# Projections in pairs, statistics apart, transfers of the end spread, a second bank in the opening, output weights later

## The chip, the cores and the metric

The kernel runs on one core of a Trainium2 chip. The core has a matrix engine (TensorE, PE in the profile; PEld is its weight load), a vector engine (VectorE, DVE), a scalar engine (ScalarE, ACT), a general one (GpSimd, POOL) and a queue that issues transfers (SyncE, SP). Each works through its own list in order; waits between them go over semaphores. The metric is device time in microseconds (us), lower is better: the median of three runs was 3494.31 us (3493.81 to 3497.04).

## The reference

Two batches `b` of 2048 rows and 512 features go through two layers. The first is a state-space block with a feed-forward part. The second is attention with 16 heads of 32 features, without an MLP in what is returned:

```python
h = _sln(hidden, w, ...)                      # layer norm, then gamma * ln + beta
qkv = (h @ Wqkv.T + bqkv).reshape(B, N, num_heads, hd, 3)
energy = jnp.einsum('bhqd,bhkd->bhqk', q, k)
att = jax.nn.softmax(energy, axis=-1) / D ** 0.5
out = jnp.einsum('bhqk,bhkd->bhqd', att, v)
out = out @ Wp.T + bp
h1 = out + hidden
h2 = _sln(h1, w, ...)
return h2 + h1
```

`_sln` takes mean and variance of each row, so the output of a row needs all heads of that row first, then the projection with `Wp`, the residual, and the norm's statistics.

## The kernel before, in words

Everything is float32. Rows are worked in chunks of 512 (`CH`), four a batch, and tiles of 128 rows. The order on every engine is the order in which the program is written out (`manual_schedule`): there is no scheduler, and lists of due work decide what is placed where.

First part. For each of eight chunks `(b, c)` the state-space block of the next chunk, the feed-forward part of this one, and the attention's features of the one behind are interleaved. The features of a chunk become keys and queries (`at_heads`, L523 to L537, product `pk`) and values (`at_values`, L539 to L551, product `pv`), and go to DRAM (`kd`, `qd`, `vd`). A key or query piece is evacuated by `halves`: ACT makes `hi`, DVE makes `lo` from the same PSUM bank and `hi`. Transposed features (`pt_tf`, L149) are evacuated by ACT into `fT`. All these pieces take their PSUM bank from `Banks.tile` (L191 to L196), which goes round the pools in `banks`; after the first part one pool of one bank, `ps_a`, is left in it. `hi` has two buffers, `lo` one.

Second part. A block `n` is a batch, a pair of heads and a chunk of queries: 2 x 8 x 4 = 64 blocks (`blocks`; in batch 1 the last chunk of the last two pairs stands at the end). A block is worked in `NP` = 8 periods `j`; for the keys it has 16 tiles of 128. Of these, 11 (`NX`) are kept: PE makes scores `s` (L753), ACT copies them to a ring buffer `x` (L764), DVE takes the running maximum `run` (L769). The maxima over the other five tiles come from `m` (L778, one buffer) and `top` (L783). `turn_run` and `spread` (L785 to L808) make the largest values into a row and send it to all partitions by DRAM (`flat`, then `shift`). From then on POOL takes the shift off a kept tile (`take_off`, L812), or DVE makes a tile anew with the shift off (`make`, L818, `pT`), ACT takes the exponential (L823), and PE multiplies with the values and a column of ones (`weighted`, L833, `o`). Maxima run `AHEAD` = 14 periods before the exponentials. In a period PE makes one `m` pair, one or two kept tiles, at most one made tile, and the `o` of two tiles. At the end of a block `raw` goes to DRAM: sums to `sd` (L846), weighted values to `od` (L849).

The opening is where the two parts meet, periods -22 to -5: the pieces that are left of the first part (`left`: eight `at_values`, four `at_features`, eight `at_heads`) are placed between the maxima of blocks 0 and 1. In period -4 the pools of the first part are closed; the PSUM of the second is `ps` (pool `ps2`): two double banks `s`, one double bank `m`, one bank `pt` for transposes, and one for `o`.

Output tiles. When all heads of a chunk are done, sums are inverted (`fetch_sums`, `invert`) and each of its row tiles is fetched, divided by its sums on POOL, projected, and normed. For batch 0 this is spread over the blocks of batch 1, two tiles in three blocks: with `k` a multiple of 8, group by group of 128 features `project` is placed in periods `k+5`, `k+6`, `k+7` (before the `o` products) and `k+8` (at the period's start), then `residual` and `statistics` at the end of `k+8`, `gain` in `k+9`. The projection `py` uses the bank `pt`. For batch 1 a tile comes every two periods, with all four groups together; its row `y` has one buffer (L972), from which the result is sent out (L980).

The last chunk has its own path: `end_fetch` (L990 to L1012) loads what its tiles need into free ring buffers in period `j-1` with `j` = 504: products of heads (`o`), divisors (`by`, one transfer a head, `end_divisors`), rows of `x2` (`h`) and a turned copy of the last group of output weights (`w`, with `turn`). `end_divide`, `end_begin`, `end_project` and `end_last` use them from period 507 on. The output weights `wp` are loaded in period 2 and scaled on POOL in period 8 (L1219 to L1222).

All transfers named here are issued by SP in program order. The program's transfers rotate through eight semaphores, and one is not issued before the one eight places earlier has landed.

Of the kernel before, what the change touches and what calls it, by code (L numbers as in the profile page):

```python
# [11 lines left out]
HALF = mybir.dt.float32r  # L12
# [7 lines left out]
P = 128  # L20
# [19 lines left out]
def tile_s5_block_then_sln_attention(  # L40
# [21 lines left out]
    nc = tc.nc  # L62
    NB, L, D = x.shape
    KC = D // P
    CH = 512
    TT = CH // P
    NCH = L // CH
    FC = w1.shape[1] // P
    NH, HD = 16, 32
    NG = D // P  # L70
# [31 lines left out]
    x2 = [dpool.tile([L, D], F32, name=f"x2_{b}") for b in range(NB)]  # L102
# [4 lines left out]
    od = [dpool.tile([D, L], F32, name=f"od_{b}") for b in range(NB)]  # L107
    sd = [dpool.tile([NH, L], F32, name=f"sd_{b}") for b in range(NB)]
    invd = [dpool.tile([NH, L], F32, name=f"invd_{b}") for b in range(NB)]
# [45 lines left out]
    def halves(hi, lo, psum, bias):  # L155

        nc.scalar.activation(hi, psum, AF.Identity, bias=bias, scale=1.0)  # L157
        nc.vector.scalar_tensor_tensor(lo, psum, bias, hi.bitcast(F32), ALU.add, ALU.subtract)  # L158
# [21 lines left out]
    work1 = late.enter_context(tc.tile_pool(name="work", bufs=2))  # L180
    banks = [late.enter_context(tc.tile_pool(name="ps_a", bufs=1, space=PSUM))]
# [9 lines left out]
    class Banks:  # L191


        def tile(self, shape, dtype, name, tag=None):
            banks.append(banks.pop(0))
            return banks[-1].tile(shape, dtype, name=name, tag="ps")  # L196

    ones = Banks()

# [60 lines left out]
    for q in range(4):  # L260
        f = FC // 4
        cols = slice(q * f * P, (q + 1) * f * P)
# [260 lines left out]
    def at_heads(b, c, i):  # L523

        w, bias, dst = ((wk, V_BK, kd[b]), (wq, V_BQ, qd[b]))[i // KC]
        g, hT = i % KC, fts[b, c]
        at = slice(c * CH, (c + 1) * CH)
        pk = ones.tile([P, CH], F32, name="pk")
        for k in range(KC):
            nc.tensor.matmul(  # L530
                pk, w[:, k, g * P : (g + 1) * P], hT[:, k, :], start=k == 0, stop=k == KC - 1
            )
        hi = work1.tile([P, CH], HALF, name="hi")
        lo = work1.tile([P, CH], HALF, name="lo", bufs=1)
        halves(hi, lo, pk, vec[:, bias + g : bias + g + 1])
        nc.sync.dma_start(dst[0, g * P : (g + 1) * P, at], hi.bitcast(F32))
        nc.sync.dma_start(dst[1, g * P : (g + 1) * P, at], lo.bitcast(F32))  # L537
# [22 lines left out]
    spare = ps1.tile([P, TT, D], F32, name="spare", tag="po", bufs=1)  # L560
# [126 lines left out]
    for j in range(2 * KC):  # L687
        left.insert(TT + j, (at_heads, *order[-1], j))
# [15 lines left out]
    ring = ctx.enter_context(tc.tile_pool(name="ring", bufs=22, side="right"))  # L704
    rows_r = ctx.enter_context(tc.tile_pool(name="rows_r", bufs=2, side="right"))
    ps = ctx.enter_context(tc.tile_pool(name="ps2", bufs=1, space=PSUM, side="right"))
    dsum = ctx.enter_context(tc.tile_pool(name="dsum", bufs=3, space=DRAM))

    ISQ = 1.0 / float(D) ** 0.5
# [10 lines left out]
            opens.append(n)  # L720
    pair_of = [pairs.index((b, p)) for b, p, _ in blocks]
    kst, qst, shifts, runs, tops = {}, {}, {}, {}, {}
    kept, probs, outs, ends = {}, {}, {}, {}

    def load_k(i):
        b, p = pairs[i]
# [258 lines left out]
    LB, LC = NB - 1, NQ - 1  # L985

    def spare(name):
        return ring.tile([P, 2, CH], F32, name=name, tag="x")

    def end_fetch():  # L990
        cols = slice(LC * CH, (LC + 1) * CH)
        ends["o"] = [spare("o01"), spare("o23")]
        ends["by"] = [spare("by01"), spare("by23")]
        ends["h"] = [spare("h01"), spare("h23")]
        w = spare("w")
        ends["w"], ends["turn"] = w[:, 0, :], w[:, 1, :P]
        for g in range(NG - 1):
            nc.sync.dma_start(ends["o"][g // 2][:, g % 2, :], od[LB][g * P : g * P + P, cols])
            end_divisors(range(4 * g, 4 * g + 4))
        for t in range(TT):  # L1000
            at = slice((LC * TT + t) * P, (LC * TT + t + 1) * P)
            nc.sync.dma_start(ends["h"][t // 2][:, t % 2, :], x2[LB][at, :])
        nc.gpsimd.tensor_copy(ends["turn"], ident)

        for to, of in ((0, 2), (1, 0), (2, 1), (3, 3)):
            nc.sync.dma_start(
                ends["w"][HD * to : HD * to + HD, :], wp[HD * of : HD * of + HD, NG - 1, :]
            )
        for to, of in ((0, 1), (3, 2)):
            nc.gpsimd.tensor_copy(  # L1010
                ends["turn"][:, HD * to : HD * to + HD], ident[:, HD * of : HD * of + HD]
            )  # L1012

    def end_fetch_more():
        cols = slice(LC * CH, (LC + 1) * CH)
        nc.sync.dma_start(ends["o"][1][HD : 3 * HD, 1, :], od[LB][D - P : D - P // 2, cols])

    def end_divisors(heads, shift=0):
        cols = slice(LC * CH, (LC + 1) * CH)
        for j in heads:  # L1020
            at = slice(HD * (j % 4 + shift), HD * (j % 4 + shift) + HD)
            nc.sync.dma_start(
                ends["by"][j // 8][at, j // 4 % 2, :], invd[LB][j : j + 1, cols].to_broadcast([HD, CH])
            )

    def end_divide(g, rows=slice(0, P)):
        o, by = ends["o"][g // 2][rows, g % 2, :], ends["by"][g // 2][rows, g % 2, :]
# [77 lines left out]
    NP = 8  # L1105
# [19 lines left out]
    def after(j, what, *args):  # L1125

        due.setdefault(j, []).append((what, args))

    def closing(j, what, *args):

        due.setdefault(j + 0.5, []).append((what, args))
# [13 lines left out]
    for b in range(NB):  # L1145
        for c in range(NQ):
            j = NP * (blocks.index((b, NPAIR - 1, c)) + 1) + 1
            if (b, c) == (LB, LC):
                most, rest = slice(0, NH - 4), slice(NH - 4, NH - 2)
                j = NP * (N - 1)  # L1150
                after(j - 5, fetch_sums, b, c, most)
                after(j - 3, invert, b, c, most)
                after(j - 1, end_fetch)
                after(j + 1, end_fetch_more)
                after(j + 1, fetch_sums, b, c, rest, 32)
                after(j + 4, invert, b, c, rest, 32)
                after(j + 5, end_divisors, range(NH - 4, NH - 2), 1)
                for g in range(NG - 1):
                    after(j + 3 + g, end_divide, g)
                for e in (1, 2):  # L1160
                    after(j + 8, end_divide, NG - 1, slice(HD * e, HD * e + HD))
                after(j + 6, end_begin, 0)
                for g in range(NG - 1):
                    after(j + 6 + g // 2, end_project, 0, [g])
                continue
            after(j, fetch_sums, b, c)
            after(j + 2, invert, b, c)
            if c == 0:
                after(j + 2, last_rows, b) if b == LB else after(NP * (NPAIR * NQ * (b + 1) + 2), last_rows, b)
            for t in range(TT):  # L1170
                qt = c * TT + t
                if b == LB:
                    k = j + 3 + 2 * t
                    after(k, fetch, b, qt)
                    after(k + 2, divide, b, qt)
                    after(k + 3, project, b, qt)
                    after(k + 3, residual, b, qt)
                    after(k + 3, statistics, b, qt)
                    after(k + 4, deviation, b, qt)
                    after(k + 5, last_norm, b, qt)  # L1180
                    after(k + 6, last_close, b, qt)
                else:

                    k = NP * (NPAIR * NQ * (b + 1) + 2 + 3 * qt // 2)
                    after(k, fetch, b, qt)
                    after(k + 3, divide, b, qt)
                    for g in range(3):
                        closing(k + 5 + g, project, b, qt, (g,))
                    after(k + 8, project, b, qt, (3,))
                    closing(k + 8, residual, b, qt)  # L1190
                    closing(k + 8, statistics, b, qt)
                    closing(k + 9, gain, b, qt)
                    after(k + 11, turns, b, qt)
                    closing(k + 12, scaled, b, qt)
                    after(k + 14, close, b, qt)
# [5 lines left out]
    def block_at(j):  # L1201
        n, i = divmod(j, NP)
        return (n, i) if 0 <= n < N else (None, i)

    for j in range(FIRST, NP * N + 2):
        if j == OPEN:
# [5 lines left out]
            rows = ctx.enter_context(tc.tile_pool(name="rows", bufs=2))  # L1212
# [3 lines left out]
            for v in vst:  # L1216
                nc.gpsimd.memset(v[:, :, 1, :], 1.0)
            wp = fixed.tile([P, KC, D], F32, name="wp")
        if j == 2:  # L1219
            nc.sync.dma_start(wp, w_pT.rearrange("(k p) f -> p k f", p=P))  # L1220
        if j == NP:
            nc.gpsimd.tensor_scalar(wp, wp, ISQ, None, ALU.mult)  # L1222
        run_due(j)
        n, i = block_at(j + AHEAD)
        todo = list(keeps[i]) if n is not None else []
        now, k = block_at(j)
# [24 lines left out]
        n, i = block_at(j + 1)  # L1251
# [4 lines left out]
        n, i = block_at(j - 1)  # L1256
# [59 lines left out]
```

## Time and profile before

| | |
|---|---|
| median of three runs | 3494.31 us |
| profiled execution, own time | 3497.08 us |
| its span, first to last instruction | 3495.3 us |
| mean granted TensorE clock | 0.989 |
| first part, to the last `po` product | about 1384 us |
| opening, to the first transposed row of maxima | 1384 to 1473 us |
| plain blocks of the second part | 28.5 us each |
| blocks 33 to 57, with output tiles of batch 0 | 29.5 to 35.5 us each |
| blocks 61 and 62, with output tiles of batch 1 | 49.1 and 48.6 us |
| chain that ended last, by engine | PE 73%, DVE 13%, ACT 8%, DMA 2%, POOL 2% |

How it is read: busy time is given by engine and by line; a group's line names what is written and read. In the timeline, each row has its start in us from the span's start, its duration, engine, line and tile; the bracket says how long the engine was idle before it and what released it. The waits list who waited for whom: us in total, times, longest. Matmuls overlap, so the distance between starts, not the duration, is what PE spends: a projection of one group is two rows, 0.43 us apart each.

### The profile page before, as it was taken

How to read it: one execution, taken by the hardware profiler on the slowest of the kernel's cores; microseconds unless marked ns; L12 is line 12 of the kernel's file. 1: busy time of each engine (PE TensorE's matmuls, PEld its weight loads, DVE VectorE, ACT ScalarE, POOL GpSimd, SP SyncE). 2: the span in 40 equal slices, each digit the busy share in tenths (PEclk: the TensorE clock that was granted, in tenths of full speed). 3: DMA queues.
4: the chain of work that ended last, by engine and by line, in shares of the span. 5: the costliest groups of instructions: out<-in, count | busy, mean ns of one | idle time of the engine just before them, and what ended most of it. 6: DMA issues, size and time to landing. Idle time of an engine off the chain costs nothing.

```text
span 3495.3 us, 34359 instructions
## 1 busy us (share of the span) xinstructions
PE 3343.7 (96%) x11764; PEld 1509.3 (43%) x11764; DVE 2153.1 (62%) x2976; ACT 1942.2 (56%) x2208; POOL 2137.7 (61%) x1162
## 2 busy tenths in 40 slices
PE   7999999999999999799999999999999999999997
PEld 4444444444444444444444444444444444444432
DVE  6232232323232311488888888888888888888885
ACT  2111111111111011389999999999888888888862
POOL 4223131313131310189899989998889888889986
PEclk8999999999999999999999999999999999999999
DMA  8001111111111112322223232323233233233233
GB/s 301 1 30 42 43 42 43 42 48 39 46 39 37 39 36 66 115 67 68 62 57 72 66 74 51 74 67 74 61 91 86 70 86 83 67 84 81 56 104 105
DMA packets 201638, 237.06 MB, mean 68 GB/s; under 512 B 89786, under 2 KB 118970, under 8 KB 197368
## 3 DMA queue, kind: packets, MB, share of 16 engines
q1 hardware_dynamic: 201464, 234.87, 24.6%
q8 instruction: 93, 1.52, 0.2%
q14 instruction: 81, 0.66, 0.1%
HBM read 166.77 MB, written 67.76 MB: 67 GB/s over the span
## 4 chain that ended last, share of the span: by engine, by line
PE 73%; DVE 13%; ACT 8%; DMA 2%; issue 2%; POOL 2%; SPq 0%; DVEq 0%; ACTq 0%; POOLq 0%
PE o L833 15%; PE ph L487 13%; PE po L500 13%; PE s L753 10%; DVE run L769 9%; PE pk L530 6%; ACT x L764 4%; PE pv L542 3%; PE py L904 3%; PE m L778 3%; PE pt_run L789 2%; PE pu L421 2%; ACT x L823 1%; ACT pT L823 1%; PE pt_tf L149 1%
## 5 line engine op out<-in xcount | busy, mean ns | idle before, releaser
L812 POOL TENSOR_TENSOR x<-x,shift 128x1024 f32<-128x1024 f32 x704 | 1654.1, 2390 | 159.9 <-DMA shift<-flat 135.8
L764 ACT COPY x<-s 128x1024 f32<-128x1024 f32 x704 | 692.4, 1012 | 212.8 <-PE s L753 211.6
L769 DVE TENSOR_TENSOR run<-s,run 128x1024 f32<-128x1024 f32 x576 | 703.0, 1220 | 82.0 <-ACT x L764 59.0
L823 ACT ACTIVATE x<-x 128x1024 f32<-128x1024 f32 x704 | 739.6, 1060 | 14.7 <-POOL x L812 14.5
L833 PE MATMUL o<-x,v 128*64 128x512 f32 x2816 | 720.4, 613 | 0.0
L753 PE MATMUL s<-qs,ks 128*128 128x512 f32 x2048 | 670.0, 422 | 50.4 <-DVE run L769 44.9
L487 PE MATMUL ph<-fT,w_sb 128*128 128x512 f32 x1024 | 463.1, 596 | 0.0
L500 PE MATMUL po<-w_sb,hid 128*128 128x512 f32 x1024 | 460.3, 592 | 0.0
L753 PEld LDWEIGHTS s<-qs,ks 128*128 128x128 f32 x2048 | 335.2, 189 | 274.0 <-DVE run L769 173.8
L783 DVE TENSOR_REDUCE top<-m 128x1 f32<-128x640 f32 x512 | 417.7, 816 | 40.7 <-PE m L778 38.1
L818 DVE TENSOR_TENSOR pT<-s,shift 128x1024 f32<-128x1024 f32 x320 | 389.5, 1217 | 57.6 <-PE s L753 57.6
L491 ACT ACTIVATE hid<-ph,vec 128x512 f32<-128x512 f32 x128 | 88.0, 687 | 595.7 <-PE ph L487 595.7
L823 ACT ACTIVATE pT<-pT 128x1024 f32<-128x1024 f32 x320 | 339.4, 1060 | 67.3 <-DVE pT L818 67.3
L158 DVE SCALAR_TENSOR_TENSOR lo<-pk,vec,hi 128x512 fp32r<-128x512 f32 x64 | 48.1, 751 | 505.2 <-ACT hi L157 500.0
L833 PE MATMUL o<-pT,v 128*64 128x512 f32 x1280 | 333.5, 600 | 13.4 <-ACT pT L823 13.4
L833 PEld LDWEIGHTS o<-x,v 128*64 128x64 f32 x2816 | 157.3, 136 | 316.7 <-issue 214.4
L487 PEld LDWEIGHTS ph<-fT,w_sb 128*128 128x128 f32 x1024 | 193.1, 192 | 228.7 <-issue 228.7
L778 PE MATMUL m<-ks,qs 128*128 128x320 f32 x1024 | 261.5, 337 | 29.1 <-DVE top L783 25.7
L434 POOL TENSOR_TENSOR m<-m,m 128x512 f32<-128x512 f32 x8 | 13.1, 1641 | 449.7 <-DVE m L432 449.7
L500 PEld LDWEIGHTS po<-w_sb,hid 128*128 128x128 f32 x1024 | 190.7, 190 | 221.4 <-issue 221.4
L157 ACT ACTIVATE hi<-pk,vec 128x512 fp32r<-128x512 f32 x64 | 44.0, 687 | 394.1 <-PE pk L530 389.5
L510 POOL TENSOR_TENSOR x<-x,gated 128x512 f32<-128x512 f32 x32 | 39.6, 1270 | 354.3 <-DVE gated L509 354.3
(253 smaller groups left out, 2781.8 us busy)
## 6 DMA issues: line engine op xcount, KB each, us to landing
ks<-kd SPq DMA_DIRECT2D x128, 256.0 KB
qs<-qd SPq DMA_DIRECT2D x512, 64.0 KB
shift<-flat SPq DMA_DIRECT2D x64, 512.0 KB
x<-in_x SPq DMA_DIRECT2D x8, 1024.0 KB
w_sb<-in_w SPq DMA_DIRECT2D x8, 1024.0 KB
x<-x SPq DMA_DIRECT2D x8, 1024.0 KB
kd<-hi SPq DMA_DIRECT2D x32, 256.0 KB
kd<-lo SPq DMA_DIRECT2D x32, 256.0 KB
```

The costliest lines, as they stand in the source:

```text
L487: nc.tensor.matmul(ph, w1_sb[:, k, f * P : (f + 1) * P], fts[b, c][:, k, :], start=k == 0, stop=k == KC - 1)
L500: nc.tensor.matmul(pos[b, c][:, t, :], hid[:, t * P : (t + 1) * P], w2_sb[:, f, :], start=f == 0, stop=f == FC - 1,)
L530: nc.tensor.matmul(pk, w[:, k, g * P : (g + 1) * P], hT[:, k, :], start=k == 0, stop=k == KC - 1)
L753: nc.tensor.matmul(s[:, e, :], kst[pair_of[n], e][:, kt * P : (kt + 1) * P], qst[n][:, e, :], start=True, stop=True,)
L764: nc.scalar.copy(x, s)
L769: nc.vector.tensor_tensor(runs[n], s, kept[n, 0] if kt == 1 else runs[n], ALU.max)
L778: nc.tensor.matmul(m[:, i, :YW], qst[n][:, e, t * P : (t + 1) * P], kst[pair_of[n], e][:, k : k + YW], start=True, stop=True,)
L783: nc.vector.tensor_reduce(tops[n][:, j, 0:1], m[:, :, :YW], AX.XY, ALU.max, negate=True)
L812: nc.gpsimd.tensor_tensor(x, x, shifts[n], ALU.add)
L818: nc.vector.tensor_tensor(x, s, shifts[n], ALU.add)
L823: nc.scalar.activation(x, x, AF.Exp)
L833: nc.tensor.matmul(outs[n][64 * e : 64 * e + 64, :], v[:, kt, e : e + 2, :], x[:, e, :], start=first, stop=final,)
```

## The change

- `Banks.tile`: the pool `ps2` is appended to `banks`, with the tag `pt`, so the pieces of the opening go in turn to `ps_a` and to the bank `pt`.
- `lo` gets the two buffers of its pool.
- Batch 0's tiles: two groups of the projection in period `k+5` and two in `k+6`, all at the period's end; `residual` at the end of `k+7`, `statistics` at the end of `k+8` as before.
- `end_fetch` is cut in three. `end_sums(g)` loads `o` and `by` of one group, in periods 502, 503 and 504. `end_weights` makes `w` and `turn` in 505, `end_x` loads `h` in 506. The divisors of four heads are one transfer with a repeated source instead of four, the two of the last heads one instead of two, and the four of `h` become two.
- `wp` is loaded in period 22 and scaled in period 32.

```diff
@@ Banks.tile
-            return banks[-1].tile(shape, dtype, name=name, tag="ps")
+            return banks[-1].tile(shape, dtype, name=name, tag="pt" if banks[-1].name == "ps2" else "ps")
@@ at_heads
-        lo = work1.tile([P, CH], HALF, name="lo", bufs=1)
+        lo = work1.tile([P, CH], HALF, name="lo")
@@ after the pool ps2
+    banks.append(ps)
@@
-    def end_fetch():
+    def end_sums(g):
+        if g % 2 == 0:
+            ends["o"].append(spare("o4"))
+            ends["by"].append(spare("by4"))
         cols = slice(LC * CH, (LC + 1) * CH)
-        ends["o"] = [spare("o01"), spare("o23")]
-        ends["by"] = [spare("by01"), spare("by23")]
+        nc.sync.dma_start(ends["o"][g // 2][:, g % 2, :], od[LB][g * P : g * P + P, cols])
+        end_divisors(g, 4)
+
+    def end_x():
         ends["h"] = [spare("h01"), spare("h23")]
+        at = slice(LC * CH, (LC + 1) * CH)
+        rows = x2[LB][at, :].rearrange("(i t p) d -> p i t d", p=P, t=2)
+        for i in range(2):
+            nc.sync.dma_start(ends["h"][i], rows[:, i, :, :])
+
+    def end_weights():
         w = spare("w")
         ends["w"], ends["turn"] = w[:, 0, :], w[:, 1, :P]
-        for g in range(NG - 1):
-            nc.sync.dma_start(ends["o"][g // 2][:, g % 2, :], od[LB][g * P : g * P + P, cols])
-            end_divisors(range(4 * g, 4 * g + 4))
-        for t in range(TT):
-            at = slice((LC * TT + t) * P, (LC * TT + t + 1) * P)
-            nc.sync.dma_start(ends["h"][t // 2][:, t % 2, :], x2[LB][at, :])
...
-    def end_divisors(heads, shift=0):
+    def end_divisors(g, heads, shift=0):
         cols = slice(LC * CH, (LC + 1) * CH)
-        for j in heads:
-            at = slice(HD * (j % 4 + shift), HD * (j % 4 + shift) + HD)
-            nc.sync.dma_start(
-                ends["by"][j // 8][at, j // 4 % 2, :], invd[LB][j : j + 1, cols].to_broadcast([HD, CH])
-            )
+        nc.sync.dma_start(
+            ends["by"][g // 2][HD * shift : HD * (shift + heads), g % 2, :],
+            invd[LB][4 * g : 4 * g + heads, cols].unsqueeze(1).to_broadcast([heads, HD, CH]),
+        )
@@ placement of the end
-                after(j - 1, end_fetch)
-                after(j + 1, end_fetch_more)
+                for g in range(NG - 1):
+                    after(j - 2 + g, end_sums, g)
+                after(j + 1, end_weights)
+                after(j + 1, end_sums_more)
+                after(j + 2, end_x)
...
-                after(j + 5, end_divisors, range(NH - 4, NH - 2), 1)
+                after(j + 5, end_divisors, NG - 1, 2, 1)
@@ placement of batch 0's tiles
-                    for g in range(3):
-                        closing(k + 5 + g, project, b, qt, (g,))
-                    after(k + 8, project, b, qt, (3,))
-                    closing(k + 8, residual, b, qt)
+                    for g in range(NG):
+                        closing(k + 5 + g // 2, project, b, qt, (g,))
+                    closing(k + 7, residual, b, qt)
                     closing(k + 8, statistics, b, qt)
@@ output weights
-        if j == 2:
+        if j == 2 * NP + 6:
             nc.sync.dma_start(wp, w_pT.rearrange("(k p) f -> p k f", p=P))
-        if j == NP:
+        if j == 4 * NP:
             nc.gpsimd.tensor_scalar(wp, wp, ISQ, None, ALU.mult)
```

More of the change, by code (lines that the diff above doesn't have):

```diff
@@ L722, in tile_s5_block_then_sln_attention @@
     kst, qst, shifts, runs, tops = {}, {}, {}, {}, {}
-    kept, probs, outs, ends = {}, {}, {}, {}
+    kept, probs, outs, ends = {}, {}, {}, {"o": [], "by": []}
     def load_k(i):
@@ L1012, in end_fetch, with end_sums_more @@
             )
-    def end_fetch_more():
+    def end_sums_more():
         cols = slice(LC * CH, (LC + 1) * CH)
         nc.sync.dma_start(ends["o"][1][HD : 3 * HD, 1, :], od[LB][D - P : D - P // 2, cols])
-    def end_divisors(heads, shift=0):
+    def end_divisors(g, heads, shift=0):
         cols = slice(LC * CH, (LC + 1) * CH)
-        for j in heads:
-            at = slice(HD * (j % 4 + shift), HD * (j % 4 + shift) + HD)
-            nc.sync.dma_start(
-                ends["by"][j // 8][at, j // 4 % 2, :], invd[LB][j : j + 1, cols].to_broadcast([HD, CH])
-            )
+        nc.sync.dma_start(
+            ends["by"][g // 2][HD * shift : HD * (shift + heads), g % 2, :],
+            invd[LB][4 * g : 4 * g + heads, cols].unsqueeze(1).to_broadcast([heads, HD, CH]),
+        )
     def end_divide(g, rows=slice(0, P)):
```

## The prediction

> **What bounds the kernel now.** I read the page first, then the waits of TensorE (PE) by stretch, then the timeline where a wait is large, then the waits of the SyncE queue (SP).
>
> ```profile
> span 3495.3 us, 34359 instructions
> PE 3343.7 (96%) x11764; PEld 1509.3 (43%) x11764; DVE 2153.1 (62%) x2976; ACT 1942.2 (56%) x2208; POOL 2137.7 (61%) x1162
> ```
>
> PE is the bound over the whole, so the change is worth the PE idle time it removes, plus slow-clock time that this idle brings. Four places.
>
> Opening, 1384 to 1475 us: the last pieces of the feed-forward part are worked off beside the first keeps of the attention. Waits of PE there (us in total, times, longest):
>
> ```profile
> PE pk L530 <- DVE lo L158: 9.4, 7, 1.6
> PE pv L542 <- ACT vt L547: 3.2, 3, 1.8
> PE pt_tf L149 <- ACT fT L150: 2.9, 2, 1.9
> ...
> PE pv L542 <- DVE lo L158: 0.3, 1, 0.3
> ```
>
> Every piece waits for the evacuation of the one before: there is one bank. Together 15.8 us.
>
> Block 1, timeline:
>
> ```profile
> 1513.18 5.37 POOL L1222 TENSOR_SCALAR wp<-wp 128x2048 f32<-128x2048 f32 x1
> ...
> 1521.03 1.06 ACT L823 ACTIVATE x<-x 128x1024 f32<-128x1024 f32 x1 [4.51 <-POOL x L812]
> ...
> 1524.30 1.22 PE L753 MATMUL s<-qs,ks 128*128 128x512 f32 x2 [3.94 <-DVE run L769]
> ```
>
> The scaling of `wp` on POOL makes ACT, then PE, idle. The issues of `sd<-raw` close the blocks: 1516.5, 1552.2, 1580.7, 1609.2. Block 1 takes 35.65 us, the plain ones 28.52: a loss of 7.1, of which 3.9 is the idle; the rest goes with a granted clock of 0.50 in 1524 to 1528.
>
> Batch 0's output tiles, 2490 to 3230, PE's waits and one tile:
>
> ```profile
> PE m L778 <- DVE top L783: 21.0, 15, 1.4
> ```
>
> ```profile
> 2790.93 0.69 DVE L914 TENSOR_TENSOR py<-py,xr 128x512 f32<-128x512 f32 x1
> ...
> 2795.07 0.56 PE L778 MATMUL m<-ks,qs 128*128 128x320 f32 x2 [1.40 <-DVE top L783]
> ...
> 2796.86 1.94 PE L833 MATMUL o<-x,v 128*64 128x512 f32 x4
> ...
> 2822.40 0.82 DVE L783 TENSOR_REDUCE top<-m 128x1 f32<-128x640 f32 x1 [1.74 <-PE m L778]
> ```
>
> Residual and statistics stand together in DVE's queue after the runs of period 8; the next `top` is late and `m` has one buffer: 1.4 us once a tile. In three tiles (about 2540, 2796 and 3086) the clock drops after it; four `o` matmuls take 1.94 instead of 1.08. The last line shows DVE idle ahead of period 8's own `top`.
>
> End:
>
> ```profile
> 3415.48 0.43 SPq L998 DMA_DIRECT2D o<-od  x1
> ...
> 3430.07 0.53 SPq L980 DMA_DIRECT2D out<-y  x1
> ...
> 3433.88 0.69 DVE L973 TENSOR_TENSOR y<-z,g_row 128x512 f32<-128x512 f32 x1 [10.87 <-DMA out<-y]
> ...
> 3439.01 1.98 PE L833 MATMUL o<-pT,v 128*64 128x512 f32 x4 [8.69 <-ACT pT L823]
> ```
>
> `end_fetch` issues 3+12+4+4 = 23 transfers from 3415.48 to 3429.97. `out<-y`, whose data POOL had ready at 3421.55, is behind them; `y` has one buffer, so DVE's next `y` waits, and the `pT` behind it, and PE.
>
> **The Trainium skill.** "Perfetto Trace Analysis", Matmuls, says that independent groups should rotate through PSUM banks so that one's evacuation overlaps the next's matmuls; the 1.56 us gaps of `pk` agree. "TensorE: Matmul & The Clock Gate", What's actually happening, says that the clock halves after an idle window of about 3.4 us that runs free; the halves after 3.94 and, phase permitting, after 1.40 us of idle agree. "DMA: Bandwidth & Descriptors", Why a DMA increments its semaphore by 16 and not by 1, says that a transfer uses as many engines (up to 16) as divide both slowest dimensions: the merged `by` (4 heads outermost) would use 4. With Specifications' 27 GiB/s an engine, 256 KB are an estimated 2.3 us plus latency; no trace shows it yet.
>
> **The change part by part.**
>
> Two banks in the opening. Removed: 15.8 us of waits. Kept: `pk` needs all four `fT`. From the fourth `pv` ACT has three copies (1.0 each) and four `fT` (0.78) to do, 6.1 us; PE's own work there is about 1.0 shorter. New: the second bank is that of `pt_run`. In the order, a `pv` now stands after `pt_run` 0 and has to wait for its `top` (vt 0.69 and top 0.68, less 1.0 of m and s between them: 0.35), and `pt_run` 1 waits for that `pv`'s evacuation (latency 0.2, vt 0.69: 0.95). 15.8 - 1.0 - 1.3 = 13.5. The order of ACT, DVE and SP is the same in this stretch; DVE has 3.5 us of work per two pieces (lo 0.75 twice, top 0.81, run 1.22) against PE's 7.9 (eight issues of 0.43 a piece, m and s 1.1). Bounds: 5 if the writes of `hi` and `lo` (the first took up to 5 us to land) hold the two buffers, 15 if nothing new waits. The second buffer of `lo` removes one cause, a wait at 1421.00. Taken: -13.5.
>
> `wp` later. Load and scaling move to periods 22 and 32, POOL's queue keeps two take-offs of block 4 ahead of the scaling. Block 1's loss of 7.1 goes. In block 4 POOL starts at 1599.78, two take-offs at 2.39 end at 1604.6, the scaling at 1610.0, the third at 1612.4; ACT wants it at 1609.08. So ACT is 3.3 late, PE about 0.6 less (4.51 against 3.94 in block 1): 2.7, and a slow window of 2.5 with it: 5.2. The cover is POOL's early start, 1.2 us better than in block 1 because no `ks` loads follow the shift. On SP the 1.32 us issue of `wp` comes right after block 3's `shift` and ahead of the `v` loads, which have 9 periods; sharing the engines could hold `shift` up as `ks` loads do (5.4 us of POOL idle against 2.8), at most 0.4 late for ACT. Bounds: 7.1 gain (hidden) to 1 loss. Taken: -1.9.
>
> Projections. PE work is the same, 8 issues of 0.43; two groups stand in period 5 and two in 6. The residual moves ahead of `top` in period 8. There DVE is idle for 1.74; the last group no longer delays `m`, which takes 0.86 off; 0.88 is left, the residual needs 0.69, so it is hidden. If that cover is gone it costs 0.69. After the runs DVE then has 0.69 less: `m` waits 0.7, not 1.4. 16 x 0.69 = 11.0. Without 1.4 us gaps I expect the three slow windows to go; each costs four or eight `o` at double time, some 1.7: 5.1, of which I take 4. Bounds: 0 to -16. Taken: -15.
>
> End. Now 2 issues in each of periods 502 and 503, so `out<-y` is ready to go at its data, 3421.6, and lands by 3425.4 (3.8 as above). The next `y` can run at 3425.5 (its `z` ends at 3425.41), the residual at 3427.1 (PE's `py`), after statistics `pT` at 3429.2 and its exponential to 3431.5; PE resumes at 3431.6, not 3439.0: 7.4. The slow clock after it (`o` 1.98 for 1.08, `py` 4.25 for 3.70) goes: 1.4. In exchange the following `out<-y` stands behind `o`, `by`, the four `w` (0.6 each) and waits for `od<-raw`; I put it at 3432.5, landed at 3436.3, 1.3 after its `y` is wanted, where before that wait was 4.1. The two 512 KB `h` have four periods. POOL's `turn` copies (0.64) move two periods down, under the same slack. Bounds: 2 to 11. Taken: -8.7.
>
> Sum: -13.5 - 1.9 - 15 - 8.7 = -39.1. The profiled execution took 3497.08 (its span and 1.8 around it): 3458. The median is 2.8 below it: 3455, which I round up for parts counted whole: **3456**.
>
> **Rivals.**
>
> A. The opening finds another wait: the landings of `hi`/`lo` or ACT's order set the pace. For it: in the first pieces `hi` and `lo` were put down to `kd<-lo`, 4.6 and 5.2 us. Against: from 1425 on they follow at once. Gain 5 instead of 13.5: 3464.
>
> B. The end's wait comes back at the next `out<-y`, behind `w` and `od` on SP; for it, eleven issues stand between. Gain 2: 3463.
>
> C. Slower: DVE's gap in period 8 is smaller than the residual, because `m` is held by something other than the last group. Then `top` is late in period 8 and again in 10, and every tile's idle sits in one window and halves the clock: 0.7 + 1.7 a tile on top of now, 16 x 2.4 = 38 lost, against 24 gained elsewhere: 3508. It decides from 1.5 us a tile. Against it: the 1.74 ends at `m` in every tile that I looked at.
>
> D. `wp` is wholly hidden in block 4 and all slow windows go: 3450. E. The projections move nothing, since PE then waits for the statistics just as long: 3470.
>
> **How the numbers follow.** Forecast as worked 0.48 (3448 to 3461), A 0.13, B 0.12, D 0.10, E 0.07, C 0.05, other losses 0.05. From 3444 to 3474 lie the forecast, A, B, D and E, 0.9 together, less some for the tails of each: 8 in 10. A measurement here tells about 0.2%, 7 us. Faster 0.91, same 0.03, slower 0.06.
>
> **What would show it.** `pk` waiting for `lo` gone in the opening, with 0.3 and 1 us at `pt_run` in their place, and `pt_neg` of block 0 some 13 us earlier; block 1 at 28.5 and block 4 at 33 to 34 us; `m <- top` at about 0.7 a tile and `py<-py,xr` ahead of `top`; `out<-y` issued within 1 us of POOL's `y` near 3390, and no PE wait over 3 us there. I am wrong if block 4 loses as much as block 1 did, if the `top` of period 8 starts late, or if SP waits for landings where it now waits for issues.

## The result: 3494.06 to 3459.12 us, and the profile after

| | before | after |
|---|---|---|
| median, four runs each | 3494.06 us | 3459.12 us |
| lowest and highest | 3492.89, 3497.04 | 3457.48, 3463.26 |
| ratio, 95% interval | | 0.9901 (0.9883 to 0.9918) |
| profiled execution, its span | 3497.08, 3495.3 us | 3459.56, 3457.8 us |

The page's head for the kernel after:

```profile
span 3457.8 us, 34348 instructions
...
PE 3335.5 (96%) x11764; PEld 1508.3 (44%) x11764; DVE 2151.7 (62%) x2976; ACT 1939.8 (56%) x2208; POOL 2137.8 (62%) x1162
```

PE issues as many matmuls as before and is busy 8.2 us less (3343.7 against 3335.5). That fits less time at the low clock: from 1500 us on, the stretches at a granted clock of 0.50 add up to 34.7 us before and 17.4 after, and half of the difference is 8.7. The other 29.3 of the 37.5 us are idle time of PE that is gone. Below, line numbers from L754 on are one higher than before.

To see where the 37.5 us come from, I cut the span at the first `sd<-raw` issue of each block (SP, which closes the block). "Opening" is the time of block 0's; "4" is the sum of blocks 1 to 4; the end is block 62 and the rest after it.

| us | opening | 1 to 4 | 33 to 57 | 62 | rest | span |
|---|---|---|---|---|---|---|
| before | 1516.5 | 121.2 | 805.7 | 48.6 | 60.6 | 3495.3 |
| after | 1502.2 | 119.0 | 789.6 | 43.0 | 61.3 | 3457.8 |
| difference | -14.3 | -2.2 | -16.1 | -5.6 | +0.7 | -37.5 |
| predicted | -13.5 | -1.9 | -15 | -8.7 for both | | -39.1 |

The columns that are left out, blocks 5 to 32 and 58 to 61, differ by 0.3 us at most between the two.

The opening: waits of PE from 1384 to 1462 us, in us in total, times, longest, after:

```profile
PE m L779 <- DVE top L784: 1.7, 2, 1.3
PE s L754 <- DVE run L770: 1.3, 2, 0.8
PE pt_run L790 <- DVE vt L550: 0.8, 1, 0.8
PE pv L542 <- DVE gated L509: 0.7, 1, 0.7
PE pt_tf L149 <- ACT fT L150: 0.6, 1, 0.6
PE pv L542 <- DVE top L791: 0.2, 1, 0.2
```

No `pk` waits for its predecessor's `lo` any more. The two waits at the shared bank are there, 0.8 and 0.2, where 0.95 and 0.35 were expected. `pt_neg` of block 0 stands at 1457.18 instead of 1472.62.

The output weights, timeline after: the scaling on POOL, ACT's exponential behind it, PE's scores behind that.

```profile
1583.45 5.37 POOL L1230 TENSOR_SCALAR wp<-wp 128x2048 f32<-128x2048 f32 x1
...
1591.30 1.06 ACT L824 ACTIVATE x<-x 128x1024 f32<-128x1024 f32 x1 [3.58 <-POOL x L813]
...
1594.56 0.73 PE L754 MATMUL s<-qs,ks 128*128 128x512 f32 x2 [3.00 <-DVE run L770]
```

Block 1 takes 28.50 us (before 35.65), block 4 takes 33.42 (before 28.52). So the loss has moved and is smaller, as the sum had it: ACT's wait is 3.58 and PE's 3.00, for the expected 3.3 and 2.7.

The tiles of batch 0, waits of PE from 2420 to 3210:

```profile
PE s L754 <- DVE run L770: 16.2, 52, 0.7
PE m L779 <- DVE top L784: 10.7, 16, 0.7
```

Sixteen waits of 0.7, once a tile; before they were 1.4 (21.0 in 15 waits, and one of 1.4 that the list puts down to `qs`), so 11.7 us are gone here. PE's busy time in blocks 33 to 57 falls from 763.5 to 759.0, and the three stretches of 3.4 us at a clock of 0.50 that stood in these blocks are gone. The two together make up the 16.1 us.

The end, timeline after, SP's issues of `out<-y` and DVE's next `y`:

```profile
3388.31 0.34 SPq L981 DMA_DIRECT2D out<-y  x1
...
3395.68 0.69 DVE L974 TENSOR_TENSOR y<-z,g_row 128x512 f32<-128x512 f32 x1 [5.18 <-DMA out<-y]
...
3400.82 1.46 PE L834 MATMUL o<-pT,v 128*64 128x512 f32 x4 [3.00 <-ACT pT L824]
...
3404.47 0.40 SPq L981 DMA_DIRECT2D out<-y  x1
...
3406.74 0.69 DVE L974 TENSOR_TENSOR y<-z,g_row 128x512 f32<-128x512 f32 x1 [5.33 <-DMA out<-y]
```

The first output is now issued when POOL has it (its `y` runs from 3387.01 to 3388.28). But DVE can write `y` again only 7.4 us after this issue; 3.8 were expected. The next output, ready at 3399.68, goes out at 3404.47: four `w` (4.26 us on SP) and an `o` (1.37) stand ahead. PE's wait there is 3.00, where it was 8.69. The low clock behind it has not gone:

```profile
3402.20 4.97 PE L905 MATMUL py<-wp,o 128*128 128x512 f32 x8
```

These eight matmuls took 4.25 before and 3.70 at the full clock; here a stretch of 3.4 us at 0.50 begins at 3401.4.

The merged `by` also holds SP itself up, since a transfer is not issued before the one eight places earlier has landed. Waits of the queue, 3390 to 3425 us:

```profile
SPq L997 <- DMA by<-invd: 3.3, 1, 3.3
SPq L1013 <- DMA by<-invd: 1.9, 1, 1.9
```

The first is the third `o` of the last chunk (issued at 3395.18), the second the fourth `w`; the merged `by` that they wait for were issued at 3384.47 and 3395.57. So 1.9 of the 4.26 us of `w` are a wait for a landing, not issuing.

### The profile page after: what moved, and what is told of

Read it like the earlier page. It is cut to its first block, busy times and chain, and to the rows that moved or that the text cites. A ratio compares the mean times of both kernels' runs of the same rounds, so it can differ in the third digit from the quotient of the medians.

```text
span 3457.8 us, 34348 instructions
## 1 busy us (share of the span) xinstructions
PE 3335.5 (96%) x11764; PEld 1508.3 (44%) x11764; DVE 2151.7 (62%) x2976; ACT 1939.8 (56%) x2208; POOL 2137.8 (62%) x1162
## 4 chain that ended last, share of the span: by engine, by line
PE 73%; DVE 14%; ACT 8%; issue 2%; DMA 1%; POOL 1%; SPq 0%; DVEq 0%; ACTq 0%; POOLq 0%
PE o L834 15%; PE ph L487 13%; PE po L500 13%; PE s L754 10%; DVE run L770 10%; PE pk L530 6%; ACT x L765 4%; PE pv L542 3%; PE m L779 3%; PE py L905 2%; PE pt_run L790 2%; ACT pT L824 2%; ACT x L824 2%; PE pu L421 2%; PE pt_tf L149 1%
## 5 line engine op out<-in xcount | busy, mean ns | idle before, releaser
L754 PE MATMUL s<-qs,ks 128*128 128x512 f32 x2048 | 669.5, 421 | 51.3 <-DVE run L770 45.2
L754 PEld LDWEIGHTS s<-qs,ks 128*128 128x128 f32 x2048 | 334.4, 189 | 275.4 <-DVE run L770 149.7
```

What stands on the lines that cost most here:

```text
L754: nc.tensor.matmul(s[:, e, :], kst[pair_of[n], e][:, kt * P : (kt + 1) * P], qst[n][:, e, :], start=True, stop=True,)
```

## The experiments

My theory after the result: the four parts are independent and add up; three of them work as the prediction says, and the end falls short because the merged `by` delays the output issued behind it. The ledger for them all (us):

| kernel | opening | 1 to 4 | 33 to 57 | 62 | rest | span | median |
|---|---|---|---|---|---|---|---|
| banks alone | 1501.5 | 120.3 | 804.2 | 49.1 | 61.4 | 3479.3 | 3481.46 |
| projections alone | 1517.0 | 121.7 | 790.0 | 48.5 | 61.2 | 3481.0 | 3480.37 |
| end alone | 1515.5 | 121.5 | 805.4 | 43.1 | 64.5 | 3492.7 | 3493.81 |
| residual late | 1501.0 | 118.7 | 806.3 | 44.2 | 62.0 | 3475.2 | 3477.66 |
| `by` one a head | 1502.0 | 119.0 | 789.0 | 43.9 | 61.3 | 3458.2 | 3461.03 |
| sums early | 1501.9 | 119.2 | 791.4 | 46.2 | 65.1 | 3466.7 | 3468.63 |
| `y` in the ring | 1502.7 | 118.7 | 789.4 | 44.2 | 63.0 | 3460.8 | 3461.56 |
| `wp` in four | 1501.0 | 114.1 | 789.4 | 44.4 | 62.2 | 3455.0 | 3457.75 |
| additions on DVE | 1500.2 | 119.0 | 789.2 | 44.8 | 63.2 | 3459.4 | 3463.51 |
| that and ring | 1499.7 | 118.7 | 790.5 | 45.2 | 64.2 | 3461.1 | 3463.76 |
| that and `wp` in four | 1499.9 | 114.1 | 789.1 | 45.1 | 63.3 | 3455.4 | 3459.47 |
| `by` and `w` on SP, `wp` in four | 1500.6 | 114.1 | 789.3 | 42.0 | 64.5 | 3454.6 | 3456.28 |

One caution comes out of the table. Kernels with the same end do not agree on it: after, end alone, residual late and `wp` in four have 104.2, 107.7, 106.1 and 106.6 us for block 62 and the rest together. The old end (before, banks alone, projections alone) has 109.2, 110.5 and 109.6. So the end's part is 109.8 - 106.2 = 3.6 us over these executions, and differences under about 3 us there say nothing. Two parts of this scatter can be seen. In the four kernels named, `shift` is issued 23.8, 24.0, 25.5 and 25.0 us after block 61 closes, ahead of every transfer that the change moved, and block 62 takes 43.0, 43.1, 44.2 and 44.4. And PE is busy 82.3 us in the end of after, at a mean clock of 0.94, but 83.3 to 83.7 at 0.92 in the other three. The other columns repeat within about 3 us where the program is the same, and block 61 alone, in all fourteen kernels, within 0.03 (49.05 to 49.08).

That the parts add up is seen from the kernels with one part each. Their medians are 14.3 (banks), 15.4 (projections) and 1.9 (end) below the kernel before, taken beside them; each is known to 3 to 6 us. `wp` alone was not run: from banks alone to after, blocks 1 to 4 fall from 120.3 to 119.0, so it is worth about 1.3 there. The sum is 32.9, for 34.9 measured.

**Two banks alone** (on the kernel before):

```diff
-            return banks[-1].tile(shape, dtype, name=name, tag="ps")
+            return banks[-1].tile(shape, dtype, name=name, tag="pt" if banks[-1].name == "ps2" else "ps")
-        lo = work1.tile([P, CH], HALF, name="lo", bufs=1)
+        lo = work1.tile([P, CH], HALF, name="lo")
+    banks.append(ps)
```

> The kernel before with the second PSUM bank of the opening alone (and the second buffer of lo). Theory, parts that add up: the opening's gain is all its own, so block 0 closes 14.3 us earlier (1502.2), block 1 still loses its 7.1, and the whole is 14 us faster: 3480. Rival, the parts share something (the clock, a DMA queue): block 0 closes less than 10 us earlier when the output weights are still loaded in period 2, and the whole gains under 8.

Measured: ratio 0.9957 (0.9942 to 0.9971); block 0 closes at 1501.5, 15.1 us earlier. The opening's part is all its own, also with the weights still loaded in period 2.

**Projections alone** (on the kernel before):

```diff
-                    for g in range(3):
-                        closing(k + 5 + g, project, b, qt, (g,))
-                    after(k + 8, project, b, qt, (3,))
-                    closing(k + 8, residual, b, qt)
+                    for g in range(NG):
+                        closing(k + 5 + g // 2, project, b, qt, (g,))
+                    closing(k + 7, residual, b, qt)
```

> The kernel before with the projections two groups a period and the residual before the statistics' period, nothing else. Theory: m waits for top 0.7 us instead of 1.4 once a tile, the slow windows go, blocks 33 to 57 take 16 us less together, the whole 16 less: 3478. Rival: part of those 16 us belongs to the different place of the free-running clock window after the opening moved; then under 11 us here.

Measured: ratio 0.9954 (0.9937 to 0.9970); blocks 33 to 57 take 790.0, 15.7 less. The rival falls: this gain needs no other place of the opening's end. That place does decide a little: in banks alone two stretches of low clock fall into blocks 33 to 57 instead of three, and these blocks take 1.5 us less.

**End alone** (on the kernel before): `end_sums`, `end_x`, `end_weights`, `end_sums_more` and the merged `end_divisors` with their periods, as in the change.

> The kernel before with the spread and merged transfers of the end alone. Theory: blocks 61 and 62 and the last one together take 5 us less (3489), with a wait of about 5 us of DVE for a landing out<-y near where it was 10.9. Rival, the recorded sum of the prediction: 8.7 less (3485), the landing being slowed by something from the other parts.

Measured: ratio 0.9995 (0.9986 to 1.0003). Block 62 is 5.5 shorter, the rest 3.9 longer, of which the scatter above may hold most. DVE waits 5.43 for a landing output, 7.29 us after its issue. The 8.7 of the prediction are not there; the time alone cannot tell this part from nothing.

**Residual late** (on the changed kernel):

```diff
-                    closing(k + 7, residual, b, qt)
+                    closing(k + 8, residual, b, qt)
```

> The changed kernel with the residual put back beside the statistics (closing of k+8), the groups still two a period, all of them ahead of period 8. Theory, the residual's place carries it: m waits 1.4 us for top again once a tile, 11 us lost, and 2 to 5 more where the clock window falls on them: 3470 to 3475. Rival, the pairing carries it (no last group between the run and m in period 8): at most 3 us lost, 3460 to 3462.

Measured: ratio to before 0.9947; blocks 33 to 57 take 806.3, so all of the gain is gone. Waits of PE in this stretch (2419 to 3225):

```profile
PE m L779 <- DVE top L784: 22.4, 16, 1.4
PE s L754 <- DVE run L770: 18.0, 53, 1.3
```

The 16.7 us are 11.7 at `m`, 1.8 at `run`, and 2.6 of PE's busy time (761.6 against 759.0), with two stretches of 3.4 us at a clock of 0.50; 0.6 is left over. So the pairing gains nothing by itself: it lets the residual stand ahead of the statistics' period, and that gains.

**One transfer a head for `by`** (on the changed kernel, still spread):

```diff
-        nc.sync.dma_start(
-            ends["by"][g // 2][HD * shift : HD * (shift + heads), g % 2, :],
-            invd[LB][4 * g : 4 * g + heads, cols].unsqueeze(1).to_broadcast([heads, HD, CH]),
-        )
+        for i in range(heads):
+            at = slice(HD * (i + shift), HD * (i + shift) + HD)
+            nc.sync.dma_start(
+                ends["by"][g // 2][at, g % 2, :], invd[LB][4 * g + i : 4 * g + i + 1, cols].to_broadcast([HD, CH])
+            )
```

> The changed kernel with the divisors of the last chunk in one transfer a head again (four 64 KB ones of 32 rows for one 256 KB one), still spread over the periods. Theory, the merged transfer keeps few DMA engines busy for long and the output that is issued behind it lands late: that output now lands about 4 us after its issue instead of 7.4, DVE's wait for it falls from 5.2 to about 2, block 62 takes 40 to 41.5 us instead of 43.0. Rival, the bytes in front of it decide, or SP's three more issues a group (1.4 us) eat it up: the wait stays within 1 us of 5.2 and block 62 within 0.8 of 43.0. In time at most 3 us, so the trace decides.

Measured: 3461.03, ratio to before 0.9904. Timeline of SP and DVE at the two outputs:

```profile
3387.63 2.75 SPq L1029 DMA_DIRECT2D by<-invd  x4
3390.48 0.37 SPq L981 DMA_DIRECT2D out<-y  x1
```

```profile
3392.81 0.69 DVE L974 TENSOR_TENSOR y<-z,g_row 128x512 f32<-128x512 f32 x1 [2.92 <-POOL x L813]
...
3406.28 0.69 DVE L974 TENSOR_TENSOR y<-z,g_row 128x512 f32<-128x512 f32 x1 [6.97 <-DMA out<-y]
```

The delay is shown: with the same bytes ahead of it, the output issued directly behind four small `by` lets DVE go on at most 2.33 us after its issue, not 7.4. "DMA: Bandwidth & Descriptors" in the Trainium skill says under Rules for kernel authors that an outermost dimension of fewer than 16 confines a whole transfer to at most that many engines; the merged `by` has 4, and the two landings agree with that. The run with additions on DVE (below) shows it directly: there SP issues nothing from 3385.13 to 3391.65, and the last four transfers before are two `o` and two merged `by`. A window in the second half of that time, and then the same window of this run, read as follows; the last two figures are the busy share of the 16 DMA engines and GB/s:

```profile
3388.50:3391.50 3.00, 2.07 (x5) 0.46 (x5) 2.97 (x2) 2.82 (x4) 2.94 (x3) 0.58 0.26 94
3388.50:3391.50 3.00, 2.14 (x7) 0.78 (x8) 1.21 (x6) 3.00 (x4) 3.00 (x3) 1.00 0.84 210
```

A share of 0.26 is 4.2 of 16 engines, as the 4 rows of the merged `by` would have it.

But the expected 2 us of gain are not there: block 62 stays at 43.9. The output is issued 2.2 us later: 1.3 of that are SP's extra issues (its data are there at 3389.14), and 0.9 is data that come later, after a `shift` issued 0.5 later than in the changed kernel, ahead of every transfer that differs. The next output is issued at 3403.78, behind `w` and `o`, so that wait grew from 5.33 to 6.97, although the four `w` now take 2.78 us on SP instead of 4.26.

**Sums early** (on the changed kernel): the same transfers four periods earlier.

```diff
-                after(j - 5, fetch_sums, b, c, most)
-                after(j - 3, invert, b, c, most)
+                after(j - 9, fetch_sums, b, c, most)
+                after(j - 7, invert, b, c, most)
-                    after(j - 2 + g, end_sums, g)
+                    after(j - 6 + g, end_sums, g)
```

> The changed kernel with the sums, their inversion and the transfers of o and by of the last chunk four periods earlier, in the same form. Theory as in the run with one transfer a head: nothing of theirs is in flight when the output of period 504 is issued; it lands in about 4 us, DVE's 5.2 us wait falls to about 2, block 62 takes 40 to 41.5 us. If instead the tiles' own fetches (o, four by, xr of the same period) hold it, it still lands after 6 to 8 us and block 62 stays at 43. Block 61 may lose up to 2 us if an output there now stands behind them.

Measured: 3468.63, slower than the change; block 62 and the rest 111.3. A miss for both. Five outputs now make DVE wait (20.1 us; 14.2 in three waits in the changed kernel), and the transfer of `shift` is late for POOL. Waits of POOL, 3340 to 3435:

```profile
POOL x L813 <- DMA shift<-flat: 5.2, 1, 5.2
```

**`y` in the ring** (on the changed kernel): buffers that are free by then, for the last four tiles.

```diff
-        y = work.tile([P, D], F32, name="y", bufs=1)
+        if qt < (LC - 1) * TT:
+            y = work.tile([P, D], F32, name="y", bufs=1)
+        else:
+            if qt % 2 == 0:
+                ends["y"] = spare("y4")
+            y = ends["y"][:, qt % 2, :]
```

> The changed kernel with the outputs y of the last four tiles before the final chunk in buffers of the ring that are free by then (two tiles a buffer), so that none of them waits for a transfer to leave. Theory, the single buffer of y is what the end still waits for: the three waits of DVE for out<-y (5.2, 5.3 and 3.7 us) go, PE's 4.5 us for pT and 1.0 for o go nearly all, block 62 and what follows take 4 to 5.5 us less: 3454. Rival, another wait takes its place (the residual for py, z for its scale): at most 2 us less.

Measured: 3461.56, no gain; the theory that the one buffer is what the end waits for falls. No `y` waits for a transfer, but PE waits for other things. Waits of PE, 3340 to 3470:

```profile
PE o L834 <- ACT pT L824: 6.2, 5, 1.4
PE py L905 <- POOL o L892: 3.7, 2, 2.7
PE py L905 <- POOL x L813: 1.1, 1, 1.1
```

The divided `o` of the tiles, POOL's work, is the next that is late.

**`wp` in four pieces** (on the changed kernel):

```diff
-        if j == 4 * NP:
-            nc.gpsimd.tensor_scalar(wp, wp, ISQ, None, ALU.mult)
+        if j in (4 * NP, 5 * NP, 6 * NP, 7 * NP):
+            g = j // NP - 4
+            nc.gpsimd.tensor_scalar(wp[:, g, :], wp[:, g, :], ISQ, None, ALU.mult)
```

> The changed kernel with the scaling of the output weights in four pieces of 128x512, one each in blocks 4 to 7, instead of one of 128x2048 in block 4. Theory, POOL has 2.2 us to spare in each block (eleven take-offs of 2.39 in 28.5): every piece of about 1.3 is hidden, block 4 falls from 33.4 to 28.5, the whole is 4.9 less: 3454. Rival, POOL's spare time is not where the pieces stand: each of the four blocks loses 0.5 to 1.3, and nothing or up to 2 us is gained.

Measured: 3457.75, ratio to before 0.9897 (0.9880 to 0.9914). Timeline of POOL:

```profile
1582.00 1.50 POOL L1231 TENSOR_SCALAR wp<-wp 128x512 f32<-128x512 f32 x1
1583.58 9.41 POOL L813 TENSOR_TENSOR x<-x,shift 128x1024 f32<-128x1024 f32 x4
```

Block 4 takes 28.52, block 5 takes 29.47 (0.94 more). The gain of 4.0 us is plain in the blocks; in the time it is under what a few runs tell apart, and 2.3 of it went again in the end's scatter.

**Additions on DVE** (on the changed kernel; then with `y` in the ring, then with `wp` in four):

```diff
-        nc.gpsimd.tensor_tensor(h, h, ending[b][1], ALU.add)
-        nc.gpsimd.tensor_tensor(y, y, h, ALU.add)
+        add = nc.vector if qt > TT else nc.gpsimd
+        add.tensor_tensor(h, h, ending[b][1], ALU.add)
+        add.tensor_tensor(y, y, h, ALU.add)
```

> The changed kernel with the two last additions of the last seven tiles before the final chunk (residual plus t_row, and y plus that) on DVE instead of POOL. The first theory of the end, y's one buffer behind slow landings, has fallen: with free buffers for y nothing was gained. New theory, POOL's own queue sets the end from period 502 on: it works from 3377 to 3424 with three gaps under 1 us, and PE's waits for pT and for o only pass its lateness on. POOL loses 2.55 a tile, DVE gets 1.4 and has 40% idle there: block 62 takes 39.5 to 41 us instead of 43 to 44.4, the rest 59 to 60.5 instead of 61 to 63, 4 to 6 us less in all. Rival, DVE's chain (z, y, residual, statistics, pT) sets it: the 1.4 us a tile are added to that chain and nothing is gained, or up to 3 are lost.

> The same with the outputs y of the last four tiles in free ring buffers too. If POOL was the first limit and y's buffer the next, this gains 2 to 3 us more than the additions on DVE alone; if out<-y, issued 2.5 us earlier from DVE, has landed in time, the two are within 1 us of each other in block 62 and the rest together.

> The changed kernel with the additions of the last seven tiles on DVE and the scaling of the output weights in four pieces in blocks 4 to 7. The two stand 1,700 us apart and add: 4 for the weights (block 4 at 28.5, block 5 about 1 longer, as measured alone) and 4 to 6 for the end: 3450. If the additions gain nothing, 3455.

Measured: 3463.51, 3463.76 and 3459.47; block 62 and the rest take 108.0, 109.4 and 108.4. No gain: 1.8 to 3.2 us above the 106.2 with the additions on POOL; the ring adds nothing. The run does not test POOL's load cleanly, because the additions got longer. Timeline of the first of the three, POOL and DVE:

```profile
3387.99 2.36 POOL L813 TENSOR_TENSOR x<-x,shift 128x1024 f32<-128x1024 f32 x1
3388.14 2.75 DVE L980 TENSOR_TENSOR xr<-xr,t_row 128x512 f32<-128x512 f32 x1
...
3390.28 0.76 POOL L1011 COPY w<-ident 128x128 f32<-128x128 f32 x1
```

And the durations of this addition for six of the seven tiles (minimum, median, maximum in ns):

```profile
L980 DVE TENSOR_TENSOR xr<-xr,t_row x6: 673/1679/2748, 3368.3 to 3422.5; 128x512 f32<-128x512 f32 x6
```

It ends 0.5 us after POOL's take-off does. "SBUF — State Buffer" in the Trainium skill says under SBUF: two separate sides that a DVE operation with two operands in SBUF and a POOL operation that reads SBUF exclude each other, the second waiting until the first is done; these times agree, and the expectation had left it out. POOL also stood idle 15.0 us in all for the tiles' `by`, so it did not hold the end throughout in this run.

**The last run** (on the changed kernel): `by` one a head, `wp` in four, and

```diff
-                after(j + 1, end_weights)
-                after(j + 1, end_sums_more)
+                after(j + 3, end_weights)
+                after(j + 3, end_sums_more)
```

> The changed kernel with one transfer a head for the divisors of the last chunk (with that alone, the first late output landed at most 2.3 us after its issue instead of 7.4, but the next stood behind w and o on SP), the turned weights w and the last o of the final chunk issued in period 507 instead of 505, so that this next output is issued at its data, and the scaling of the output weights in four pieces (alone: block 4 4.9 us shorter, block 5 0.9 longer). Theory, SP's queue and the landings set the end: the three waits of DVE for out<-y (5.2, 5.3, 3.7) fall below 2 each, block 62 and the rest together take 99 to 102 us instead of 104 to 107, the whole about 3450. Rival, POOL sets it (47.65 us of work in the 49.9 from 3376.0 to 3425.9, in which PE has 42.1): the waits for out<-y go, others for POOL's o and x stand in their place, block 62 and the rest stay at 103 to 107, the whole 3454 to 3458.

Measured: 3456.28, ratio to before 0.9886 (0.9869 to 0.9902), the lowest of all, though its interval overlaps that of the change. Timeline of DVE:

```profile
3387.55 0.69 DVE L974 TENSOR_TENSOR y<-z,g_row 128x512 f32<-128x512 f32 x1 [2.49 <-ACT z L972]
...
3399.03 0.69 DVE L974 TENSOR_TENSOR y<-z,g_row 128x512 f32<-128x512 f32 x1 [4.68 <-DMA out<-y]
```

The first wait for a transfer is gone and block 62 is at 42.0, the lowest. The next two outputs still keep DVE waiting, 4.68 and 4.48; of the first, 3.8 pass between issue (3395.23) and landing. PE waits 3.0 for POOL's `o`; block 62 and the rest take 106.5. So the rival's numbers hold, those of SP and landings do not. In the 49.9 us from 3371.5, PE is busy 41.15 and POOL 47.16.

What stays open: which single limit holds the end. Four cures of a wait each (landing, buffer, SP's order, POOL's additions) took their wait away or shortened it, and none brought more than the scatter. POOL, almost without a gap there, fits best; it is not shown, since no run lightened it without slowing something else. Against it stands the run with the additions on DVE, where POOL waited 15.0 us and the end was no shorter.

## Why the prediction was right

3456 was predicted, 3459.12 measured, inside 3444 to 3474. By its steps:

**Opening**, -13.5 against -14.3 (and -15.1 alone): right in mechanism and size, with both new waits at `pt_run` and `pv`. Rival A, another wait, would have shown in this column; it does not. (A slip in the sum: 0.2 and 0.69 make 0.89, not 0.95; at the end 7.4 and 1.4 make 8.8, not 8.7. Neither matters.)

**`wp`**, -1.9 against -2.2: right, within what the runs can tell. Banks alone already has 0.9 of the 2.2, so the move itself is worth about 1.3. Rival D, wholly hidden, falls for this change; the four pieces come near to it.

**Projections**, -15 against -16.1: right. `m` waits 0.7 for 1.4, and the low clock's share was 4.5 us by PE's busy time, for the 4 taken. One reading was wrong. The prediction counts the half clock after gaps of 1.40 us as agreeing with an idle window of about 3.4 us. A grid is there: in every run the stretches at 0.50 begin whole multiples of 3.41 us apart. But in the 3.41 us ahead of the three in the tiles (from 2537.53, 2793.53 and 3083.66) PE was busy for 1.91, 1.91 and 1.90 us, so none of these windows was idle throughout. Another (from 2503.40), with PE busy for 1.90, was followed by no half clock. The measurement decides: gaps of 1.40 us can be followed by half the clock, and what picks the tiles stays open. Rival C (the residual makes `top` of period 8 late) and rival E (nothing moves) fall with projections alone and residual late.

**End**, -8.7 against -4.9 in the profiled execution and -3.6 over the executions: right in mechanism, but about twice what came. (By the medians of end alone it is 1.9, not clear of nothing.) Three terms were mis-sized. "Lands by 3425.4 (3.8 as above)" took the landing from an output that had no merged transfer ahead of it; it was 7.4. The prediction had worked out that the merged `by` uses 4 engines, and priced only the `by` itself, not the output queued behind it. The following output, put 1.3 us after its `y` is wanted, was 5.33 after: it was issued 4.8 us after its data. The slow clock behind PE's wait, 1.4 to be gained, stayed: `o` took 1.46 and `py` 4.97, for 1.08 and 3.70. One sign that the prediction named for being wrong is there in part: SP waits 3.3 and 1.9 us for landings of the merged `by`. Rival B named the place and the `w` and `o` on SP as the cause; it holds in part, with a gain of 4 or 5 in the traces, and of 2, as B said, in the medians of end alone.

That the total is only 3 us off owes something to chance: 3.8 too much at the end stand against 2.2 too little in the other three.

## What to carry to other kernels

When a transfer is merged, ask which engines it uses and what is issued behind it, not only how many issues it saves. Where issues wait for landings eight places earlier, a transfer that lands late also delays issues that have nothing to do with it. In the end, where POOL is busy 95% and PE 84% of 49.9 us, one removed wait mostly uncovered the next; add up each engine's work in such a stretch before you price a wait. Before work goes from POOL to DVE, look whether both then read SBUF at the same time: a 0.68 us addition was up to 2.75 long.

## What the runs showed of the hardware

- An output of 256 KB behind two 256 KB transfers with 4 outermost rows landed 6.8 to 7.5 us after its issue (in after, end alone, residual late and `wp` in four); behind the same bytes in 64 KB transfers of 32 rows, within 2.33 us (`by` one a head) and 3.30 us (the last run).
- With only such transfers left in flight, the 16 DMA engines were busy for a share of 0.26, at 94 GB/s (additions on DVE, 3388.5 to 3391.5 us).
- The stretches at a granted clock of 0.50 begin whole multiples of 3.41 us apart in every run. In before, three of them follow 3.41 us in which PE was busy for 1.90 or 1.91 us.
- An addition of two SBUF operands on DVE, 128x512, took 0.67 to 2.75 us beside POOL's take-offs. POOL's own copy of 128x128 took 0.76 us beside one, where it took 0.29 in the changed kernel.
- The end, with the same instructions, took 104.2 to 107.7 us in four kernels, while block 61 repeats within 0.03 us in all.
